# Layer 1's first keys in layer 0's last block, first loads in another order, and layer 1's queries behind feature maps and values

## The chip, the cores and the metric

The kernel runs on one core of one Trainium2 chip. The metric is the device time of one execution in microseconds, the median of several runs. The engines are named as in the profile: PE (TensorE, matmuls), PEld (its weight loads), DVE (VectorE), ACT (ScalarE), POOL (GpSimd) and SP (SyncE, which mostly issues transfers). Each engine works through a list of its own in order; it waits only for semaphores that other engines and transfers raise. Transfers can be issued by SP, by ACT and by POOL, and an issue stands in the list of its engine like any other instruction.

## The reference, cut to what matters

A stack of four layers works on x (8 batches of 256 tokens, width 512), with a context of the same shape. Every layer adds a gated attention over the context and a gated feed-forward part:

```
x = x + tanh(g_xattn[0]) * xattn0(layernorm(x), ctx)      # layer 0
x = x + tanh(g_ffn[0])   * ffn0(layernorm(x))
x = x + tanh(g_xattn[1]) * xattn1(layernorm(x), ctx, ctx) # layer 1
x = x + tanh(g_ffn[1])   * ffn1(layernorm(x))
...                                                       # layers 2 and 3

xattn0: q = w8a8(x, wq);  k = ctx @ wk.T + bk;  v = ctx @ wv.T + bv    # 16 heads of 32
        out = w8a8(softmax(q k / sqrt(32) + mask) v, wo)
        # w8a8 quantises rows of activations and of weights to 8 bits on the fly
ffn0:   8 experts of rank 64; each token uses the one with the largest logit
xattn1: q = x @ Wq.T + bq;  k = ctx @ Wk.T + bk;  v = ctx @ Wv.T + bv  # 16 heads of 32
        q' = relu(q Wqf.T);  k' = relu(k Wkf.T) * mask                 # 64 features a head
        out = (q' (k' v)) / (q' sum(k') + 1e-8)  @ Wo.T + bo           # linear attention
ffn1:   64 experts, 8 for each token, routed; and a shared MLP
```

The keys of layer 1 depend on the context alone and not on x. The change rests on this: they can be computed at any time once the context, Wk and bk are there.

## The kernel before, in words

The 2048 tokens are cut into 4 blocks (NB) of 512, two batches each, and a block into 4 tiles (TB) of 128 tokens. The width of 512 is cut into 4 chunks (KC) of 128. x stays in on-chip memory as 16 tiles (xt). A product of a 128-wide chunk of a 512x512 weight with a block is four matmuls in f32, each in two passes (line 177, helper matmul_k); such a product for all of a block is 16 matmuls, 32 passes. Results land in PSUM, in pools mm (4 buffers), tr (2, for transposes) and ac (2), and are copied out by DVE or ACT.

A scheduler orders the instructions from the order in which the program names them, with their dependencies and the pools' free buffers; so where the code says yield or step(), the author interleaves by hand, and the scheduler moves things from there.

*First loads.* The gates' two small broadcasts and their tanh are the first things on ACT's queue (lines 76 to 79). front() (line 222) then loads wq on SP, wk on ACT, x's first four tiles on SP, the first block's transposed context (load_ctxT, line 85) on ACT, wv and the biases on ACT, wo and the other tiles of x on SP. DVE quantises wq; PE transposes it and, in keys(0) (line 262), multiplies the context with wk; queries(0) (line 281) normalises and quantises x; values(0) follow.

*Layer 0.* Eight batches of attention (attend0, line 429) run one after the other. In each, 16 heads are scored four at a time, exponentiated on ACT, transposed and multiplied with the values. After each head step() (line 409) lets other work into the stream: the projection of the batch before (project), and as many pieces of others(blk) (line 363) as `due` says. others gives the experts of the block before (experts, line 303), and the queries, keys and values of the block behind. The last block has no block behind it, so there is less to interleave, and `due` grows by 0.65 a head there instead of 1.1. After the last head come what is left of the generator, the projection of the last batch, and the experts of the last block, one after the other:

```
            for _ in gen:
                pass
        for _ in proj[0]:
            pass
        for _ in experts(NB - 1, mmtile):
            pass
```

*Layer 1* (middle, line 580, loads its weights at 586 and behind). attend1 (line 657) does for each block: load the context; K, 16 matmuls; the norm of x, its transposes (norm_T), and four adds of the output bias to x on POOL (line 665); Q, 16 matmuls; then for each of the two batches kf, the keys' feature map, 64 small matmuls of 32 rows (line 687), values (8 matmuls for the batch's two tiles), qf, kv, qkv, transposes and the output projection. Here, too, step() gives room to another generator: route1 (line 799), which for every batch finished before normalises x, computes the logits, chooses experts, and writes 16 sets of rows to a table in DRAM with indirect transfers on POOL (line 906).

*Queues.* SP issues weights, contexts, x and masks in order. ACT issues biases, broadcasts and, at the start, wk, the context and wv, between its activations. POOL issues the indirect transfers and computes each norm's power (line 145), the adds of gbo and some more, all in order.

Of the kernel before, what the change touches and what calls it, by code (L numbers as in the profile page):

```python
# [20 lines left out]
P = 128  # L21
# [24 lines left out]
def flamingo_kernel(ctx: ExitStack, tc: tile.TileContext, a):  # L46
# [29 lines left out]
    nc.scalar.dma_start(gate[:, 0:4], a["g_xattn"].partition_broadcast(P))  # L76
    nc.scalar.dma_start(gate[:, 4:8], a["g_ffn"].partition_broadcast(P))
    tg = const.tile([P, 8], F32, tag="tg", name="tg")
    nc.scalar.activation(tg, gate, AF.Tanh)
# [3 lines left out]
    ctxT = {}  # L83

# [137 lines left out]
    def front():  # L222
        isd = 1.0 / float(np.sqrt(HD))
        raw = {"wq0": weight_k("wq0", "wq0")}
        wkT = weight(a["wkT0"], "wk0", eng=nc.scalar).rearrange("p (k o) -> p k o", k=KC)
        for i in range(TB):
            nc.sync.dma_start(xt[i], a["x"][ts(i, P), :])
        load_ctxT(0, "a", nc.scalar)
        wvT = weight(a["wvT0"], "wv0", eng=nc.scalar).rearrange("p (k o) -> p k o", k=KC)
# [3 lines left out]
        gbo = row("bo0", "gbo0")  # L233
        raw["wo0"] = weight_k("wo0", "wo0")
# [68 lines left out]
        def experts(blk, bank):  # L303
            A, Bw = AB
            xns = norm(blk, "f0")
            yield
            xnT = b8.tile([P, KC, BLK], F32, tag="b8", name=f"xnT_f0{blk}")
            for i in range(TB):
                transpose4(xnT[:, :, ts(i, P)], xns[i], f"f0{blk}_{i}")
                if i % 2:  # L310
                    yield
# [51 lines left out]
        def others(blk):  # L363

            if blk + 1 < NB:
                load_ctxT(blk + 1, "a")
            if blk == 0:
                gsw_ps = actile("gsw_ps")
                quantised("wo0", lambda j, s: spread(gsw_ps[:, ts(j, P)], s, f"wo{j}"))
                nc.vector.tensor_scalar(gswo, gsw_ps, tg[:, 0:1], None, ALU.mult)  # L370
                aos.append(wpool.tile([P, 2, 2, C], F32, tag="w", name="aos"))
                yield
                AB.extend([weight_k("A0", "A0"), weight_k("B0", "B0")])

            def tokens():
# [4 lines left out]
                if blk + 1 < NB:  # L380
                    yield from queries(blk + 1, actile)

            def context():
                if blk + 1 < NB:
                    yield from keys(blk + 1, actile)
                    yield from values(blk + 1, actile)

            yield from mix(tokens(), context(), 2)

# [15 lines left out]
        for blk in range(NB):  # L405
# [3 lines left out]
            def step():  # L409
                if proj and next(proj[0], 0) is not None:  # L410
                    proj.pop()
                due[0] += 1.1 if 0 < blk < NB - 1 else 0.65
# [11 lines left out]
        for _ in proj[0]:  # L424
            pass
        for _ in experts(NB - 1, mmtile):
# [153 lines left out]
    def middle():  # L580
        with ExitStack() as st:
# [4 lines left out]
            wk = weight_k("WkT1", "Wk1")  # L586
# [69 lines left out]

            def attend1(blk, step):
                load_ctxT(blk, "b")
                K = b8.tile([P, KC, BLK], F32, tag="b8", name=f"K1_{blk}")
                Q = b8.tile([P, KC, BLK], F32, tag="b8", name=f"Q1_{blk}")  # L660
                for dst, w, bias, src in ((K, wk, bk, ctxT[blk]), (Q, wq, bq, None)):
                    if src is None:
                        _, src = norm_T(blk, "a1")
                        for t in range(blk * TB, blk * TB + TB):
                            nc.gpsimd.tensor_tensor(out=xt[t], in0=xt[t], in1=gbo, op=ALU.add)
                    for j in range(KC):
                        ps = mmtile(f"qk1_{blk}_{j}")
                        matmul_k(ps, [w[:, k, ts(j, P)] for k in range(KC)], [src[:, k, :] for k in range(KC)])
                        nc.scalar.activation(dst[:, j, :], ps, AF.Identity, bias=bias[:, j : j + 1])
                        step()  # L670
                for bb in range(BLK // S):
                    nm = f"{blk}_{bb}"
                    V = la.tile([P, 2, NH, HD + 1], F32, tag="V1", name=f"V1_{nm}")
                    nc.gpsimd.memset(V[:, :, :, HD : HD + 1], 1.0)
                    kf = b8.tile([P, 2, NH * FD], F32, tag="b8", name=f"kf_{nm}")
                    qf = b8.tile([P, NH // 2, S], F32, tag="b8", name=f"qf_{nm}")

                    heads = [slice(HD * r, HD * r + HD) for r in range(4)]
                    ps = [
                        (mm if r < 2 else ac).tile([P, 2, KC, FD], F32, tag="mm" if r < 2 else "ac", name=f"kf_{nm}_{r}")  # L680
                        for r in range(4)
                    ]
                    last = None
                    for lt in range(2):
                        for j in range(KC):
                            for r in range(4):
                                one = nc.tensor.matmul(
                                    ps[r][:, lt, j, :],
                                    K[heads[r], j, ts(bb * 2 + lt, P)],
                                    fm["WkfT1"][heads[r], :],  # L690
                                    start=True,
                                    stop=True,
                                )
                                if last is not None:
                                    behind(one, last, "heads side by side")
                                last = one
                    for r in range(4):
                        for lt in range(2):
                            t = blk * TB + bb * 2 + lt
                            nc.vector.tensor_scalar(  # L700
                                kf[:, lt, :].rearrange("p (j r f) -> p j r f", r=4, f=FD)[:, :, r, :],
# [1083 lines left out]
```

## Time and profile before

| | us |
|---|---|
| median of 3 runs | 2891.76 (2890.22 to 2892.02) |
| the profiled execution | 2896.51 |
| its span, first to last instruction | 2894.5 |
| PE busy in it | 2660.6 |
| DVE busy | 1308.3 |
| POOL busy | 932.3 |
| ACT busy | 698.2 |

The stages in the trace:

| stage | from | to | us |
|---|---|---|---|
| first loads to the first scores | 0 | 51 | 51 |
| layer 0, last block's two batches | 393.9 | 507.7 | 113.8 |
| from the last output transposes to layer 1's first matmul | 507.7 | 563.4 | 55.7 |
| layer 1, block 0 | 563.4 | 650.8 | 87.4 |
| layer 1, block 1 | 650.8 | 760.8 | 110.0 |
| layer 1, block 2 | 760.8 | 877.3 | 116.5 |
| layer 1, block 3 | 877.3 | 995 | about 118 |

The page's lines give for a group of instructions their line in the code, engine, operation, output and inputs, shapes and count. In a timeline the first two numbers are start and length in us, and a bracket names the idle time of that engine just before and what ended it ("issue" if the trace shows nothing that it waited for). In a table of windows each pair is the busy time of an engine and, in brackets, its number of instructions; behind them stand the granted clock of PE (1.00 is full speed), the share of the DMA engines' time and the rate.

### The profile page before, as it was taken

The numbers are of one execution on the slowest core, as the hardware profiler recorded it, in microseconds if no ns is written. First come the engines' busy times: TensorE is split into PE (matmuls) and PEld (weight loads), VectorE is DVE, ScalarE is ACT, GpSimd is POOL, SyncE is SP. The second block draws the span as 40 slices with busy tenths as digits, with TensorE's granted clock in tenths as the row PEclk, the third lists the DMA queues.
The fourth block names the chain that finished last, engine by engine and source line by source line (L and its number), as shares of the span: only waits on it lengthen the run. The fifth ranks groups of instructions, "written<-read, shape, count | busy, mean of one in ns | idle before, by whom it ended". The sixth has DMA issues, their size and how long they took to land. (4 is left out here: it accounts for less than half of the span.)

```text
span 2894.5 us, 29839 instructions
## 1 busy us (share of the span) xinstructions
PE 2660.6 (92%) x10528; PEld 1418.6 (49%) x10543; DVE 1308.3 (45%) x3534; ACT 698.2 (24%) x1565; POOL 932.3 (32%) x840
## 2 busy tenths in 40 slices
PE   7889978898889789999999989999899998799998
PEld 3444544465555435555555434444344434355554
DVE  7666675345545432222222281557666665121111
ACT  2534344011111113333333311122222221111111
POOL 1101020205323335555555410121322233433332
PEclk9999989899899889999999999999999999999999
DMA  5000000210101129999999861112022211488885
GB/s 200 23 4 19 19 34 5 63 37 23 59 23 38 55 67 221 217 218 217 225 214 221 181 226 58 66 62 98 29 88 87 98 15 60 137 274 293 275 272 136
DMA packets 99812, 337.02 MB, mean 116 GB/s; under 512 B 22255, under 2 KB 24687, under 8 KB 91728
## 3 DMA queue, kind: packets, MB, share of 16 engines
q0 software_dynamic: 49344, 160.45, 22.9%
q1 hardware_dynamic: 47440, 169.38, 17.1%
q10 hardware_dynamic: 2880, 5.28, 0.6%
q8 instruction: 85, 1.39, 0.2%
q14 instruction: 63, 0.52, 0.1%
HBM read 284.56 MB, written 69.02 MB: 122 GB/s over the span
## 5 line engine op out<-in xcount | busy, mean ns | idle before, releaser
L177 PE MATMUL gu<-w,eb 128*128 128x352 f32 x1024 | 326.0, 461 | 0.0
L1074 POOL DMA_INDIRECT acc<-eb,who x128 | 204.6, 1598 | 198.2 <-DVE eb L98 166.9
L177 PE MATMUL h2p<-xnT_f,p 128*128 128x512 f32 x512 | 228.0, 601 | 6.0 <-issue 3.9
L177 PEld LDWEIGHTS gu<-w,eb 128*128 128x128 f32 x1024 | 185.6, 191 | 83.2 <-issue 2.3
L177 PE MATMUL o2f<-p,h 128*128 128x512 f32 x512 | 225.6, 595 | 0.7 <-ACT h L1187 0.7
L473 ACT ACTIVATE pr<-pr,n 128x256 f32<-128x256 f32 x256 | 127.9, 501 | 158.1 <-DVE n L468 152.5
L177 PEld LDWEIGHTS h2p<-xnT_f,p 128*128 128x128 f32 x512 | 97.6, 193 | 125.7 <-issue 121.1
L177 PEld LDWEIGHTS o2f<-p,h 128*128 128x128 f32 x512 | 97.0, 191 | 119.2 <-issue 115.0
L1028 POOL DMA_INDIRECT xg<-xnd,who x128 | 134.6, 1051 | 61.1 <-PE ehp L1054 26.8
L906 POOL DMA_INDIRECT table<-pay,rowi x128 | 126.7, 990 | 64.8 <-issue 37.5
L1065 PE MATMUL ed<-w,eb 128*128 128x512 f32 x256 | 120.8, 594 | 0.9 <-DVE eb L1055 0.9
L188 DVE SCALAR_TENSOR_TENSOR x<-o2f,tg,x 128x512 f32<-128x512 f32 x64 | 47.8, 748 | 162.9 <-PE o2f L177 162.9
L98 DVE COPY eb<-ed 128x512 f32<-128x512 f32 x64 | 44.3, 692 | 158.5 <-PE ed L1065 158.5
L161 PEld LDWEIGHTS tr_xg<-ident,xg 128*128 128x128 f32 x656 | 76.4, 142 | 76.2 <-issue 57.0
L1187 ACT ACTIVATE h<-h2p,b 128x512 f32<-128x512 f32 x64 | 43.1, 687 | 290.3 <-PE h2p L177 290.2
L1044 DVE SCALAR_TENSOR_TENSOR eb<-eb,slots,gu 128x176 f32<-128x176 f32 x128 | 50.3, 393 | 139.1 <-ACT eb L1043 77.5
L161 PE MATMUL tr_xg<-ident,xg 128*128 128x128 f32 x656 | 103.4, 281 | 10.3 <-DMA xg<-xnd,who 10.3
L1442 PE MATMUL g_r<-w,xgT 128*128 128x352 f32 x288 | 111.7, 469 | 0.7 <-ACT xgT L100 0.7
L1442 PE MATMUL u_r<-w,xgT 128*128 128x352 f32 x288 | 108.7, 459 | 0.0
L480 PE MATMUL pt<-ident,pr 128*128 128x128 f32 x512 | 88.0, 293 | 19.5 <-ACT pr L473 16.2
L1043 ACT ACTIVATE eb<-gu 128x176 f32<-128x176 f32 x128 | 40.7, 318 | 264.4 <-PE gu L177 264.4
L1465 PE MATMUL d_r<-w,hT_r 128*128 128x512 f32 (+1 forms) x216 | 104.2, 592 | 0.0
(403 smaller groups left out, 4806.2 us busy)
## 6 DMA issues: line engine op xcount, KB each, us to landing
w<-in_w SPq DMA_DIRECT2D x64, 960.0 KB
p<-in_p SPq DMA_DIRECT2D x64, 512.0 KB
xnd<-xn_f SPq DMA_DIRECT2D x32, 256.0 KB
acc<-xnd SPq DMA_DIRECT2D x32, 256.0 KB
more<-acc SPq DMA_DIRECT2D x32, 256.0 KB
wd<-in_wd SPq DMA_DIRECT2D x64, 96.0 KB
x<-in_x SPq DMA_DIRECT2D x16, 256.0 KB
ctxTb<-in_ctxT SPq DMA_DIRECT2D x4, 1024.0 KB
```

Of the source, the lines that this page charges most:

```text
L161: nc.tensor.transpose(ps[:, k, :], src[:, ts(k, P)], ident)
L177: one = nc.tensor.matmul(ps, lhsT[k], rhs[k], start=(k == 0), stop=(k == n - 1))
L188: return nc.vector.scalar_tensor_tensor(xt[i], ps, scale, xt[i], ALU.mult, ALU.add)
L473: nc.scalar.activation(pr[:, nt, :], pr[:, nt, :], AF.Exp, bias=n16[:, nt, h : h + 1], scale=-1.0, accum_out=s16[:, nt, h : h + 1],)
L480: nc.tensor.transpose(pt_ps[:, lt, nt, :], pr[:, nt, ts(lt, P)], ident)
L906: one = nc.gpsimd.indirect_dma_start(out=table[:, :], out_offset=bass.IndirectOffsetOnAxis(ap=row_i[:, i, j : j + 1], axis=0), in_=pay[:, ...
L1028: nc.gpsimd.indirect_dma_start(out=xg, out_offset=None, in_=xnd[:, :], in_offset=bass.IndirectOffsetOnAxis(ap=who[:, c : c + 1], axis=0), ...
L1044: nc.vector.scalar_tensor_tensor(self.h, self.h, slots[:, c, 1:2], gu[:, I1 : 2 * I1], ALU.mult, ALU.mult)
L1065: one = nc.tensor.matmul(ps[n], t.hT[rows, k, :], wd[k][rows], start=(k == 0), stop=(k == 1))
L1074: nc.gpsimd.indirect_dma_start(out=acc[n][:, :], out_offset=bass.IndirectOffsetOnAxis(ap=who[:, t.c : t.c + 1], axis=0), in_=t.x, in_offse ...
L1442: nc.tensor.matmul(ps[:, 0:I3], xTt[:, k, :], wgu[k][:, g, :], start=(k == 0), stop=(k == KC - 1))
L1465: one = nc.tensor.matmul(ps, hT[:cn, n, :], wd[n][:cn], start=(n == 0), stop=(n == 2))
```

## The change

1. First loads: the gates' transfers and tanh become a function, called behind the loads of the biases. The context of block 0 moves from ACT's queue to the head of SP's, ahead of wq; wv follows wk at once on ACT.
2. In layer 0's last block, others() loads layer 1's Wk, a copy of its bk and the contexts of blocks 0 and 1. Between the heads run layer 1's keys of block 0 and a quarter of those of block 1, and the first two pieces of the last block's experts, whose norm is now done in two halves; `due` grows by 0.9 a head in that block. The rest of block 1's keys stands between the pieces of the last projection and behind it, and then come the experts.
3. Layer 1's attend1 takes the keys of blocks 0 and 1 from there. In every block the order becomes: keys (blocks 2 and 3 only), norm, feature map and values of the first batch (context1, which holds V, kf's 64 small matmuls and the values as attend1 had them), transposes, POOL's adds, Q, and then the rest.

The arithmetic stays the same. What is new is one small transfer (the copy of bk) and one more power on POOL (the norm in halves).

```diff
     gate = const.tile([P, 8], F32, tag="gate", name="gate")
-    nc.scalar.dma_start(gate[:, 0:4], a["g_xattn"].partition_broadcast(P))
-    nc.scalar.dma_start(gate[:, 4:8], a["g_ffn"].partition_broadcast(P))
     tg = const.tile([P, 8], F32, tag="tg", name="tg")
-    nc.scalar.activation(tg, gate, AF.Tanh)
+    def gates():
+        nc.scalar.dma_start(gate[:, 0:4], a["g_xattn"].partition_broadcast(P))
+        nc.scalar.dma_start(gate[:, 4:8], a["g_ffn"].partition_broadcast(P))
+        nc.scalar.activation(tg, gate, AF.Tanh)
...
     def front():
+        wkT = weight(a["wkT0"], "wk0", eng=nc.scalar).rearrange("p (k o) -> p k o", k=KC)
+        load_ctxT(0, "a")
         raw = {"wq0": weight_k("wq0", "wq0")}
-        wkT = weight(a["wkT0"], "wk0", eng=nc.scalar).rearrange("p (k o) -> p k o", k=KC)
+        wvT = weight(a["wvT0"], "wv0", eng=nc.scalar).rearrange("p (k o) -> p k o", k=KC)
         for i in range(TB):
             nc.sync.dma_start(xt[i], a["x"][ts(i, P), :])
-        load_ctxT(0, "a", nc.scalar)
-        wvT = weight(a["wvT0"], "wv0", eng=nc.scalar).rearrange("p (k o) -> p k o", k=KC)
...
         gbo = row("bo0", "gbo0")
+        gates()
...
-        def experts(blk, bank):
+        def experts(blk, bank, halves=1):
             A, Bw = AB
-            xns = norm(blk, "f0")
-            yield
             xnT = b8.tile([P, KC, BLK], F32, tag="b8", name=f"xnT_f0{blk}")
-            for i in range(TB):
-                transpose4(xnT[:, :, ts(i, P)], xns[i], f"f0{blk}_{i}")
-                if i % 2:
-                    yield
+            n = TB // halves
+            for half in range(halves):
+                xns = norm_of(range(blk * TB + half * n, blk * TB + half * n + n), f"f0{blk}_{half}_")
+                yield
+                for i in range(n):
+                    transpose4(xnT[:, :, ts(half * n + i, P)], xns[i], f"f0{blk}_{half * n + i}")
+                    if i % 2:
+                        yield
...
             if blk + 1 < NB:
                 load_ctxT(blk + 1, "a")
+            else:
+                first1["wk"] = weight_k("WkT1", "Wk1")
+                first1["bk"] = columns("bk1", KC, "bk1a")
+                for b in range(2):
+                    load_ctxT(b, "b")
...
                 if blk + 1 < NB:
                     yield from queries(blk + 1, actile)
+                else:
+                    for _ in range(2):
+                        yield next(last_experts)

             def context():
                 if blk + 1 < NB:
                     yield from keys(blk + 1, actile)
                     yield from values(blk + 1, actile)
+                else:
+                    yield from keys1(0, actile)
+                    yield next(last_keys)
...
+        def keys1(b, bank):
+            K1 = first1["K", b] = b8.tile([P, KC, BLK], F32, tag="b8", name=f"K1_{b}")
+            for j in range(KC):
+                ps = bank(f"k1ps{b}_{j}")
+                matmul_k(
+                    ps, [first1["wk"][:, k, ts(j, P)] for k in range(KC)], [ctxT[b][:, k, :] for k in range(KC)]
+                )
+                nc.scalar.activation(K1[:, j, :], ps, AF.Identity, bias=first1["bk"][:, j : j + 1])
+                yield
+        last_experts = experts(NB - 1, mmtile, 2)
+        last_keys = keys1(1, mmtile)
...
-                due[0] += 1.1 if 0 < blk < NB - 1 else 0.65
+                due[0] += (0.65, *(NB - 2) * (1.1,), 0.9)[blk]
...
-        for _ in proj[0]:
+        for n, _ in enumerate(proj[0]):
+            if n == 1:
+                next(last_keys)
+        next(last_experts)
+        for _ in last_keys:
             pass
-        for _ in experts(NB - 1, mmtile):
+        for _ in last_experts:
             pass
...
+            def context1(blk, bb, K, step):
...
+                return kf, V
             def attend1(blk, step):
-                load_ctxT(blk, "b")
-                K = b8.tile([P, KC, BLK], F32, tag="b8", name=f"K1_{blk}")
+                if ("K", blk) in first1:
+                    K = first1["K", blk]
+                else:
+                    load_ctxT(blk, "b")
+                    K = b8.tile([P, KC, BLK], F32, tag="b8", name=f"K1_{blk}")
+                    for j in range(KC):
+                        ps = mmtile(f"k1_{blk}_{j}")
+                        matmul_k(ps, [wk[:, k, ts(j, P)] for k in range(KC)], [ctxT[blk][:, k, :] for k in range(KC)])
+                        nc.scalar.activation(K[:, j, :], ps, AF.Identity, bias=bk[:, j : j + 1])
+                        step()
+                xns = norm(blk, "a1")
+                first = context1(blk, 0, K, step)
+                xnT = b8.tile([P, KC, BLK], F32, tag="b8", name=f"xnT_a1{blk}")
+                for i in range(TB):
+                    transpose4(xnT[:, :, ts(i, P)], xns[i], f"a1{blk}_{i}")
+                for t in range(blk * TB, blk * TB + TB):
+                    nc.gpsimd.tensor_tensor(out=xt[t], in0=xt[t], in1=gbo, op=ALU.add)
                 Q = b8.tile([P, KC, BLK], F32, tag="b8", name=f"Q1_{blk}")
-                for dst, w, bias, src in ((K, wk, bk, ctxT[blk]), (Q, wq, bq, None)):
-                    if src is None:
-                        _, src = norm_T(blk, "a1")
-                        for t in range(blk * TB, blk * TB + TB):
-                            nc.gpsimd.tensor_tensor(out=xt[t], in0=xt[t], in1=gbo, op=ALU.add)
-                    for j in range(KC):
-                        ps = mmtile(f"qk1_{blk}_{j}")
-                        matmul_k(ps, [w[:, k, ts(j, P)] for k in range(KC)], [src[:, k, :] for k in range(KC)])
-                        nc.scalar.activation(dst[:, j, :], ps, AF.Identity, bias=bias[:, j : j + 1])
-                        step()
+                for j in range(KC):
+                    ps = mmtile(f"q1_{blk}_{j}")
+                    matmul_k(ps, [wq[:, k, ts(j, P)] for k in range(KC)], [xnT[:, k, :] for k in range(KC)])
+                    nc.scalar.activation(Q[:, j, :], ps, AF.Identity, bias=bq[:, j : j + 1])
+                    step()
                 for bb in range(BLK // S):
                     nm = f"{blk}_{bb}"
+                    kf, V = context1(blk, bb, K, step) if bb else first
```

## The prediction

> **What bounds the kernel now.** I read first the busy shares, then the windows by stage, the timeline of TensorE (PE) where a window showed idle time or a low clock, and last the waits of one block.
>
> The busy shares:
>
> ```profile
> PE 2660.6 (92%) x10528; PEld 1418.6 (49%) x10543; DVE 1308.3 (45%) x3534; ACT 698.2 (24%) x1565; POOL 932.3 (32%) x840
> ```
>
> PE is the bound. The change adds no matmul and removes none, so it can only move work into stretches where PE idles or runs at half clock, or out of them. Those stretches are what counts. The windows by stage (length, then busy time and instructions of PE, its weight loads, DVE, ACT, POOL; then granted clock, DMA share, GB/s):
>
> ```profile
> 394.00:451.00 57.00, 42.43 (x287) 25.62 (x293) 34.45 (x120) 23.05 (x76) 10.53 (x8) 0.85 0.02 6
> 451.00:508.00 57.00, 49.62 (x302) 26.20 (x295) 31.98 (x109) 25.21 (x81) 5.49 (x8) 0.94 0.00 1
> 508.00:520.00 12.00, 4.38 (x17) 1.81 (x16) 6.35 (x16) 0.59 (x1) 4.41 (x4) 0.59 0.51 166
> 520.00:530.00 10.00, 6.42 (x36) 5.61 (x36) 4.25 (x9) 1.17 (x2) 1.62 (x2) 0.64 0.05 18
> 530.00:540.00 10.00, 10.00 (x29) 5.75 (x28) 3.36 (x13) 0.23 (x1) 0.00 (x0) 0.66 0.00 0
> 651.00:761.00 110.00, 96.12 (x533) 58.47 (x532) 60.72 (x254) 13.81 (x24) 39.77 (x41) 0.92 0.12 39
> 761.00:877.00 116.00, 98.00 (x532) 60.29 (x531) 57.50 (x251) 13.81 (x24) 39.53 (x41) 0.88 0.09 28
> ```
>
> See: layer 0's batches 6 and 7 (394-508) have nothing left to fill with and PE is idle for 57 - 42.4 + 57 - 49.6 = 22 us; the tail behind them (508-540) is idle for 11.2 us at a clock near 0.6; layer 1's blocks idle for 14 to 18 us each.
>
> **The change part by part.** The profiled execution took 2896.51 us (span 2894.5, 2.0 around it), 4.75 us over the median of the runs, 2891.76; differences in us worked out in it are carried to the median as they are. A measurement of this kernel can tell about 0.2%, 5.8 us, from no change.
>
> *1. First loads (0-51 us).* The timeline of ACT and its queue, and of PE, from which lines are left out:
>
> ```profile
> 8.31 1.28 ACT L79 ACT_TABLE_LOAD   x1 [8.31 <-DMA gate<-in_g_ffn]
> 8.37 0.34 ACTq L87 DMA_DIRECT2D ctxTa<-in_ctxT  x1
> ```
>
> ```profile
> 16.05 2.08 PE L177 MATMUL k0ps<-ctxTa,wk 128*128 128x512 f32 x2 [3.51 <-DMA ctxTa<-in_ctxT]
> ...
> 20.58 12.99 PE L177 MATMUL k0ps<-ctxTa,wk 128*128 128x512 f32 x28
> ...
> 36.31 1.03 PE L177 MATMUL q0ps<-qxT,qT 128*128 128x512 bf16 x3
> ```
>
> ACT stands at its tanh until the gates land, and the context load is queued behind it: issued at 8.37, landed at 16.0. After, SP issues it first. It and wk, 2 MB at the rate seen (49, 209 and 234 GB/s in the first three 2 us, then about 340), land near 8.4, so the keys can start 8 us earlier. But q0ps at 36.31 waits for something else: DVE's chain from wq (landed 7.35) through quantising it, x's norm (xn ready 24.2) and quantising x. wq comes behind them: 3 MB are in near 10.9. The gates are issued behind gbo; I put them at 21 (20 to 22). Three queues feel it. ACT, in order: the copy of the second transposed quarter of wq stands behind the tanh, and only two PSUM buffers hold such transposes, so PE's fourth set waits; the keys end near 28.5 instead of 33.4. DVE: gbo's scaling by tanh (0.48 us, at 29.19 before) now stands ahead of x's norm in the built program, so xn goes from 24.2 to about 25.9 and q0ps from 36.3 to about 36.9. SP: x0 to x3 pass behind ctxT, 1 MB, about 3 us later, which is inside that 25.9. Then PE has almost only transposes from 28.5 to 36.9; if it drops to half clock there, the query matmuls (36.3 to 39.8) take up to 3.4 more. I take +2; bounds -2 (DVE's chain not late, keys gone from in front of the transposes) and +6.
>
> The Trainium skill, "TensorE: Matmul & The Clock Gate", Part 1 ("Why this matters for your kernels" sums it up), says that an idle gap of about 3 us puts PE back to half clock, and Part 4 that transposes don't count as busy. It speaks against this part. The row 508-520, idle or on transposes at 0.59, agrees with it; by the rule the head would be 0.6 + 3.4 = +4.0 instead of +2.
>
> *2. Keys of layer 1's blocks 0 and 1 in layer 0.* They are 2 x 13.90 us of PE in layer 1 (the row of 760.79 below is another such block). In the order of the built program 25 of the 32 matmuls (0.86 us each, two passes) stand before batch 7's last output transposes, 7 behind them.
>
> Batches 6-7, 113.8 us from 393.9 to 507.7: PE busy 92.0. Clocks 0.85 and 0.94 mean about 24 us at half clock, which at 80% busy wastes 9.6, so the work is 82.4 at full clock. Added: 25 x 0.86 = 21.5 and 1.1 of transposes for the first half of the experts' norm. That is 105. The two full blocks before (132-394) are busy for 237.7 of 262 us at 0.97 and 0.93: about 230 of full-clock work, 88%. At 88%, 105 takes 119.3: +5. Bounds: 95% gives 110.5, -3; 86% gives +8; if the heads' chain through ACT and DVE holds and nothing hides, +22. I take +5, as the full blocks are the nearest rows. The loads of Wk, bk (a second copy) and two contexts, 3 MB, move here on SP and ACT; the DMA share is 0.02, and they need buffers that are free by about 370, so they cost nothing; if a context came late, PE would wait up to the 8 us that 1 MB took at the start.
>
> The tail, 507.71-563.40 (55.7 us). PE's timeline:
>
> ```profile
> 511.49 1.03 PE L212 MATMUL trq_o<-identb,q_o 128*128 128x128 bf16 x8 [3.34 <-DVE q_o L206]
> 513.02 3.19 PE L177 MATMUL wo<-qT,qoT 128*128 128x512 bf16 x7 [0.49 <-DVE qoT L98]
> 523.58 3.84 PE L161 MATMUL tr_f<-ident,xn_f 128*128 128x128 f32 x16 [7.37 <-DVE xn_f L149]
> ```
>
> A chain: quantise, transpose, project, add on POOL, norm, transpose, then experts. The order after puts 7 keys matmuls (6.0) into these waits and, since half of the norm's tiles are ready, half the logits and three of the first expert matmuls. The list at full clock: output transposes 0.4, keys 6.0, quantised transposes 0.8, projection 1.7, logits 3.7, first expert matmuls 13.8, f transposes 1.1, h transposes 2.0, second ones 13.9 = 43.4. With 2.6 of idle left: 46, so -9.7. Bounds -12 (no idle) and -5 (half the idle stays). One more rstd on POOL (0.73) is in that. Where POOL is still adding, the second half's norm is late by as much.
>
> Layer 1 loses the two blocks: -27.8, certain unless something else becomes late there.
>
> *3. Queries behind feature maps and values.* PE's timeline of block 2, and PE's waits in block 1:
>
> ```profile
> 760.79 13.90 PE L177 MATMUL qk<-ctxTb,Wk 128*128 128x512 f32 x32
> 774.52 1.04 PE L161 MATMUL tr_f<-ident,xn_f 128*128 128x128 f32 x8
> 779.04 1.30 PE L161 MATMUL tr_a<-ident,xn_a 128*128 128x128 f32 x8 [3.49 <-DVE xnT_f L98]
> ...
> 789.62 15.92 PE L177 MATMUL qk<-xnT_a,Wq 128*128 128x512 f32 x32 [4.38 <-issue]
> ```
>
> ```profile
> PE kf L687 <- issue: 8.1, 8, 1.9
> ```
>
> Every block has two bursts of 16 table writes on POOL, 22 and 20 us long (656.3-678.3 and 705.7-725.8 in block 1). From about 11.5 us into a burst until 2 us after it, PE, DVE and ACT start small instructions only every 0.7 us or so, while large matmuls are not slowed. (a) In the first bursts tr_f to Q takes 10.4, 15.1 and 11.5 us for 5.0 of work (664.5, 774.5, 891.0). (b) In the second ones the 64 small matmuls of kf take 13.5 us or more instead of 2.0, and half clock behind costs values 2.75 more: about 14.2 a stall.
>
> After, block 1 has no keys; its norm and POOL's four adds of gbo (1.26 each) stand ahead of the table writes, so the second half of the burst lies on Q's large matmuls: gain 5 (0 to 7). Blocks 2 and 3 keep keys first; then kf, values, logits fill the wait ahead of tr_a: worth up to 10.6 each if kf (2 us from about 775.6) ends before the stall (about 778); if it is caught, it loses 4.7 each instead. It is close, so I weigh both by one half: (-10.6 + 4.7) / 2 = -3 each, -6 for both. The second bursts start about 8 us later against the work, on kf of the second batch again: I leave them at 0, +-4 a block, and take off 3 of the gain for block 0 and for the shift of the adds (DVE waited 5.76 and 3.03 us for POOL at 677.6 and 790). -5 - 6 + 3 = -8, bounds -28 (both waits filled, second bursts eased too) and +18 (kf caught everywhere).
>
> Layers 2 and 3 aren't touched and move along.
>
> **Sum**: +2 + 5 - 9.7 - 27.8 - 8 = -38.5: 2891.8 - 38.5 = 2853 (2858 in a profiled execution).
>
> **The rivals.**
> *The bursts are dodged.* For it: block 0, which has no burst, runs at clock 1.00 with 86.0 of 88 us busy. Against: tables are still written, 96 of them in these blocks. Layer 1 then gives -28 instead of -8: 2833.
> *The heads don't hide the keys.* For it: PE's longest wait in 394-508 is for ACT's probabilities, and ACT gets six more keys to copy out there. Against: blocks 1-2 hide as much and more. +22 in place of +5, and kf caught in blocks 2 and 3 (+9.4 in place of -6): -38.5 + 17 = -21 with the first alone, -6 with both: 2871 to 2886, about 2877.
> *Slower: a stall in new places.* One mechanism: kf, feature maps and small transposes of the new order fall into both bursts of blocks 1 to 3. Price 14.2 us each. The parts outside layer 1's blocks sum to -30.5, so it decides from 30.5 us of added stall: two more (28.4) leave it about equal, three give -30.5 + 42.6 = +12, 2904. For it: three first bursts that now hold kf. Against: in blocks 2 and 3 keys still cover the first 14 us.
> *The first loads don't do what they say, or do.* If the earlier context did bring the queries forward by the 4.9 us that the keys end earlier, the head gives -5: 2846. It lies inside the forecast's own range.
>
> **How the numbers follow.** Forecast 0.52 (own range 2840 to 2866: the bounds of the four terms drawn together), dodged 0.15, not hidden 0.18, slower 0.11, and 0.04 for the gain and the stalls cancelling. 2824 leaves about 0.04 below; 2884 leaves the slower case and most of the even one above. Faster by over 0.2% 0.85, within 0.04, slower 0.11.
>
> **What would show it.** Part 1: first k0ps near 8 to 9 us, q0ps at 36 to 38, gates near 21. Part 2: last o near 513 instead of 507.7; first layer 1 matmul about 46 us behind it; no 13.90 us of keys in blocks 0 and 1. Part 3: in blocks 2 and 3 whether kf's 64 matmuls stay together, and Q's start less than 15 us behind tr_f. The prediction is wrong if batches 6-7 lengthen by over 10 us or if kf shows waits by issue in more than three places.

## The result and the profile after

The change makes no difference that can be measured: 2893.83 us median against 2892.97 for the kernel before, a ratio of 1.0003 with a 95% interval from 0.9992 to 1.0013. 2853 had been predicted. On a second chip the ratio was 1.0014 [1.0004, 1.0023], 3.2 us slower.

The two profiled executions differ by 7.6 us (span 2894.5 and 2886.9), more than the medians do; single executions of either kernel lie up to 11 us apart. So a stage is read from several traces here. The stages, from the end of the last matmul y of layer 0 and of the output projections wo of layer 1:

| us | first scores | layer 1 starts | block 0 | block 1 | block 2 | block 3 |
|---|---|---|---|---|---|---|
| before | 51.0 | 563.6 | 87.4 | 110.0 | 116.5 | 112.9 |
| after | 52.9 | 562.7 | 84.9 | 97.6 | 119.3 | 117.4 |
| before, second chip | 50.3 | 562.8 | 87.4 | 110.2 | 109.6 | 109.6 |
| after, second chip | 53.8 | 563.5 | 84.7 | 97.4 | 120.2 | 119.9 |

What follows layer 1's attention takes 1903 to 1905 us of the span in all of them. Layer 0 takes on 27.5 us of keys and ends within 1 us of when it did. Layer 1 loses those 27.5 us of work, but its four blocks are only 7.6 us shorter on the first chip, and 5.4 us longer on the second.

The shares of the changed kernel's page, and its windows at the end of layer 0 and by layer 1's blocks (length; busy time and instructions of PE, its loads, DVE, ACT, POOL; clock, DMA share, GB/s):

```profile
PE 2665.4 (92%) x10528; PEld 1417.6 (49%) x10543; DVE 1295.2 (45%) x3535; ACT 697.1 (24%) x1565; POOL 932.9 (32%) x841
```

```profile
394.00:451.00 57.00, 46.71 (x276) 27.02 (x271) 32.12 (x114) 23.77 (x76) 9.31 (x8) 0.88 0.02 5
451.00:508.00 57.00, 51.73 (x282) 26.47 (x285) 32.52 (x113) 25.50 (x82) 5.75 (x5) 1.00 0.00 1
508.00:520.00 12.00, 12.00 (x75) 6.40 (x76) 5.21 (x10) 2.82 (x5) 0.46 (x4) 1.00 0.02 4
520.00:530.00 10.00, 9.95 (x46) 5.53 (x46) 4.84 (x14) 1.96 (x3) 4.65 (x4) 1.00 0.66 213
530.00:540.00 10.00, 8.17 (x37) 4.60 (x35) 6.00 (x19) 0.82 (x2) 1.08 (x2) 1.00 0.00 0
```

```profile
562.70:647.60 84.90, 78.62 (x479) 48.73 (x478) 46.40 (x157) 11.45 (x19) 13.83 (x13) 0.92 0.11 38
647.60:745.20 97.60, 82.04 (x501) 52.24 (x502) 50.26 (x241) 10.73 (x20) 33.41 (x36) 0.91 0.14 44
745.20:864.50 119.30, 102.11 (x534) 61.73 (x533) 54.74 (x254) 13.81 (x24) 39.46 (x41) 0.89 0.09 27
```

The holes in layer 0's tail are closed: from 508 to 540 PE is busy for 30.1 of 32 us, at full clock. The windows 394 to 508 are idle for 15.6 us instead of 22. Block 0 of layer 1, which ran at full clock with 86 of 88 us busy, is now idle for 6.3 us and at 0.92; blocks 1 and 2 are idle for 15.6 and 17.2 us.

PE's timeline shows where. (tr_a and tr_f are transposes of the normalised x, for the queries q and for route1; k and v are keys and values, kf is the keys' feature map, lgp_f are route1's logits.) In block 0:

```profile
564.58 7.13 PE L180 MATMUL v<-Wv,ctxTb 128*128 128x512 f32 x16
571.55 1.04 PE L164 MATMUL tr_a<-ident,xn_a 128*128 128x128 f32 x8
576.18 1.97 PE L164 MATMUL tr_a<-ident,xn_a 128*128 128x128 f32 x8 [3.60 <-DVE xnT_a L101]
578.83 16.02 PE L180 MATMUL q<-xnT_a,Wq 128*128 128x512 f32 x32 [0.68 <-ACT xnT_a L103]
```

The queries still wait for the norm, now behind 9 us of kf and values instead of 13.9 us of keys. The second half of the transposes waits 3.6 us for a copy on DVE, which has kf's eight copies and the values' ahead of it; then the queries run partly at half clock (16.02 for 14.0). In block 2:

```profile
745.05 13.90 PE L180 MATMUL k<-ctxTb,Wk 128*128 128x512 f32 x32
758.79 1.04 PE L164 MATMUL tr_f<-ident,xn_f 128*128 128x128 f32 x8
759.75 1.10 PE L710 MATMUL kf<-WkfT,K 32*128 32x64 f32 x26
761.63 0.42 PE L710 MATMUL kf<-WkfT,K 32*128 32x64 f32 x2 [0.78 <-issue]
...
772.54 5.21 PE L180 MATMUL v<-Wv,ctxTb 128*128 128x512 f32 x6 [0.44 <-issue]
```

The first batch's kf starts 9.2 us into the burst of table writes, is caught 10.4 us into it, and takes 12.4 us instead of 2.0, and values run at half clock behind it.

### The profile page after: what moved, and what is told of

Read it like the earlier page. It is cut to its first block, busy times and chain, and to the rows that moved or that the text cites. A ratio compares the mean times of both kernels' runs of the same rounds, so it can differ in the third digit from the quotient of the medians.

```text
span 2886.9 us, 29835 instructions
## 1 busy us (share of the span) xinstructions
PE 2665.4 (92%) x10528; PEld 1417.6 (49%) x10543; DVE 1295.2 (45%) x3535; ACT 697.1 (24%) x1565; POOL 932.9 (32%) x841
## 5 line engine op out<-in xcount | busy, mean ns | idle before, releaser
L1097 DVE SCALAR_TENSOR_TENSOR eb<-eb,slots,gu 128x176 f32<-128x176 f32 x128 | 50.3, 393 | 138.7 <-ACT eb L1096 87.7
L504 DVE CUSTOM_DVE_ANT_0 pr<-s,mask 128x256 f32<-128x256 f32 x256 | 96.8, 417 | 11.1 <-PE s L484 7.7
```

The source lines that it names most:

```text
L504: one = nc.vector.tensor_tensor_reduce(pr[:, nt, :], ps[r][:, nt, :], mask[:, nt, :], -1.0, -LOW, ALU.add, ALU.min, n16[:, nt, h : h + 1],)
L1097: nc.vector.scalar_tensor_tensor(self.h, self.h, slots[:, c, 1:2], gu[:, I1 : 2 * I1], ALU.mult, ALU.mult)
```

## Experiments

Two theories stood against each other. Theory 1: the keys taken out of layer 1 had covered the norm's chain there, so their time was not on the path. Theory 2: the new order puts small matmuls under the table writes, and that takes the gain. Each part was run alone first. The diffs show only the lines that decide.

**The first loads alone** (the gates' loads and front()'s order as in the change, nothing else).

```diff
+        wkT = weight(a["wkT0"], "wk0", eng=nc.scalar).rearrange("p (k o) -> p k o", k=KC)
+        load_ctxT(0, "a")
         raw = {"wq0": weight_k("wq0", "wq0")}
```

> Only the first loads in the changed order, on the kernel before. The theory (the queries wait for the chain from wq over x's norm, which the earlier context does not touch): first scores 1 to 3 us later than 51.0, the whole +2 us (0 to +4). The rival (the earlier context brings the first block forward): first scores near 46, the whole -5 us.

2890.84 against 2887.26: 1.0011 [1.0002, 1.0020], +3.6 us; first scores at 54.1 and layer 1's start at 566.1 in the profile. On the second chip the kernel before has its first scores at 50.3 and the changed one at 53.8, the same step. The rival falls; the theory's size holds, at the upper end of its 0 to +4.

**The keys alone** (part 2, layer 1's order as before).

```diff
+                K = first1.get(("K", blk))
+                products = []
+                if K is None:
+                    load_ctxT(blk, "b")
+                    K = b8.tile([P, KC, BLK], F32, tag="b8", name=f"K1_{blk}")
+                    products.append((K, wk, bk, ctxT[blk]))
```

> Layer 1's keys of blocks 0 and 1 in layer 0's last block, the first loads and layer 1's order as before: in those blocks the norm now stands in front of the queries with no keys beside it. Theory 1 (in layer 1 the keys had covered the norm's chain from the last addition to x, so that taking them out uncovers it): layer 0 with its tail about 0, block 0 shorter by 3 to 5 us only instead of 13.9, block 1 by 5 to 10, blocks 2 and 3 as before; the whole -8 to -15 us. Theory 2 (the changed order in layer 1 is what gives the gain back, by small matmuls under the table writes): block 0 and 1 shorter by 12 to 14 each, the whole near -28.

2887.72 against 2887.26, 1.0002 [0.9993, 1.0011]: nothing. Layer 1 starts at 562.9; block 0 takes 87.7 (87.4 before), block 1 110.7; with the keys in place, in the run of the first loads on the same chip, they take 87.4 and 110.1. Both theories expected some gain. Split by batches, block 0's first shortens from 57.6 to 51.3 and its second grows from 29.8 to 36.4; block 1's change from 66.9 and 43.3 to 59.5 and 51.2. What a first batch gains, the second gives back. In block 1 a new stall has a part in it: the first batch's kf takes 12.5 us there instead of 2.0. PE's timeline of block 0's first batch:

```profile
568.53 1.94 PE L162 MATMUL tr_a<-ident,xn_a 128*128 128x128 f32 x8 [5.62 <-DVE xn_a L150]
570.80 1.88 PE L162 MATMUL tr_a<-ident,xn_a 128*128 128x128 f32 x8 [0.34 <-DVE xnT_a L99]
573.36 14.00 PE L178 MATMUL qk<-xnT_a,Wq 128*128 128x512 f32 x32 [0.68 <-ACT xnT_a L101]
```

**The order alone** (part 3, all keys in layer 1).

```diff
+                xns = norm(blk, "a1")
+                first = context1(blk, 0, K, step)
```

> Only layer 1's queries behind feature maps and values; all four blocks compute their keys in layer 1. Theory 1 (cover of the norm gone): block 0 still has its keys, so it keeps its 87 us; blocks 1 to 3 each +3 to +5 us as in blocks 2 and 3 of the changed kernel, because the first batch's feature map now stands under the table writes; the whole +9 to +15. Theory 2 (the order alone gives back everything): +25 or more.

2918.32, 1.0108 [1.0093, 1.0124]: +31 us. Block 0 87.7 as expected, blocks 1 to 3 120.4, 119.6 and 118.2, 9 to 10 each above the 109.5 to 110.1 of the run of the first loads on the same chip. Theory 1's size was too small by more than half; the order alone costs what theory 2 said. But the parts don't add up: alone they cost 3.6, 0.5 and 31 us, together 1 to 3. Most of the difference is block 1, which takes 97.4 to 97.6 us with its keys moved and the new order, and 110.7 and 120.4 with only one of the two. PE's waits in blocks 1 and 2 with the order alone:

```profile
PE kf L674 <- issue: 18.0, 24, 1.8
PE lgp_f L177 <- DVE kf L687: 7.4, 2, 4.6
```

**The table writes held back**, on both kernels, until the last batch's norm. They then stand ahead of the experts, so only the stages are compared.

```diff
-                    for j in range(K1):
-                        one = nc.gpsimd.indirect_dma_start(
+                    if q < 2 * NB - 1:
+                        later.append((row_i, pay, i))
+                    else:
+                        table_rows(row_i, pay, i)
...
+                for rows in later:
+                    table_rows(*rows, last_rstd[0])
```

> The kernel before, with the table writes of batches 0 to 6 held back until attention of layer 1 has ended (they then stand in front of the routed experts, so the whole time grows by up to 140 us; what counts is the time from the first to the last matmul of layer 1's attention, 427 us before). If the table writes are what slows the small instructions of blocks 1 to 3: the 64 small matmuls of kf take 2.0 us everywhere and the blocks shorten from 110, 116.5 and 113 to 88 to 92 each, 427 to about 360. If they are not (a limit of the matmuls or of the waits between the engines): within 15 us of 427.

> The changed kernel with the same writes held back. If the table writes are the cause: kf takes 2.0 us everywhere, block 0 as in the changed kernel (85, since it has no table writes), block 1 about 75 to 78, blocks 2 and 3 88 to 90 each, the attention of layer 1 419 to about 335; the changed kernel then keeps some 22 to 27 us of gain in layer 1 that it loses under the writes. If not: within 15 us of 419, and no more gain than the 7.7 us that the changed kernel shows there.

Whole times 2929.43 and 2913.60. Blocks of the kernel before: 87.4, 90.7, 90.7, 90.8, 359.6 in sum; of the changed one: 84.9, 77.1, 91.6, 91.8, 345.4. The 64 matmuls of kf take 2.01 everywhere, as here in block 2 of the changed kernel:

```profile
738.37 1.04 PE L166 MATMUL tr_f<-ident,xn_f 128*128 128x128 f32 x8
739.34 2.01 PE L712 MATMUL kf<-WkfT,K 32*128 32x64 f32 x64
741.28 2.84 PE L182 MATMUL v<-Wv,ctxTb 128*128 128x512 f32 x6
```

Against the first profiled pair (426.8 and 419.2) that is 67 and 74 us less, but on another chip, where a single execution of the kernel before, with its bursts, took 2850.77 us; it has no profile here, so how large the stalls are on that chip is not known, and this pair alone doesn't show that the writes make them. The pacing below does, on one chip. Without the bursts the change gains 14.2 us in layer 1, not the 22 to 27 expected: block 1 is shorter by all of its keys (13.6), block 0 by 2.5, and the new order costs 1 in each of blocks 2 and 3.

**The writes paced**: about 1.3 at each step, each waiting for the latest large matmul, with both kernels unchanged beside them.

```diff
             def step():
                 next(gen, None)
+                pace[0] = min(pace[0] + 1.3, 2.0)
+                while later and pace[0] >= 1.0:
+                    pace[0] -= 1.0
+                    table_row(*later.pop(0), latest[0])
```

> The kernel before, unchanged, for its profile on the same chip as the next three. If the stalls under the table writes belong to the kernel and not to one chip, the 64 matmuls of kf take 13 to 14 us in the second batch of blocks 1 to 3 again and the whole stays within 0.2% of the other runs of the kernel before on this chip.

> The changed kernel, unchanged, on the same chip. If stalls as large as before: equal to the kernel before within 0.2%. If the stalls are smaller on this chip than where it was profiled first, the changed kernel is faster by up to the 14 us by which the runs with the writes held back differed in layer 1.

> The changed kernel with the table writes of batches 0 to 6 not in bursts of 16 but about 1.3 at a step, each waiting for the latest large matmul. If what throttles the small instructions is the density of the writes (a reserve of about 100 instructions, refilled between the writes): kf near 2 to 4 us everywhere, layer 1's attention 419 to 350 to 375, the whole -40 to -65 us. If every write slows them, however spread: the same sum of stall in other places, the whole within 10 us of the changed kernel.

> The same pacing on the kernel before. If the density counts: layer 1's attention 427 to 365 to 385, the whole -40 to -60 us; the paced changed kernel would then be faster than this by 14 us or more, the gain that the changed kernel lost under the bursts. If not: within 10 us of the kernel before.

Against the 2888.60 of the kernel before on this chip: before 2887.29, after 2891.75 (1.0014), paced before 2844.10 (0.9854 [0.9837, 0.9870]), paced after 2828.91 (0.9798 [0.9781, 0.9814]). So bursts of writes are the cause of most of the stall: layer 1's attention takes 375.6 instead of 416.8 us in the kernel before and 360.3 instead of 422.2 in the changed one. Each write by itself is not. Pacing changes the density of the writes and also moves them beside large matmuls; the runs do not separate the two. Under pacing the changed kernel is 15.2 us faster than the other: the gain that the bursts had taken. In the changed kernel's block 2, PE and POOL while kf runs, in 3.1 us instead of 12.4 or 10.2, with a write starting inside it:

```profile
744.22 2.08 PE L710 MATMUL kf<-WkfT,K 32*128 32x64 f32 x51
746.62 0.69 PE L710 MATMUL kf<-WkfT,K 32*128 32x64 f32 x13 [0.31 <-issue]
```

```profile
745.20 1.23 POOL L855 DMA_INDIRECT table<-pay,rowi  x1 [0.30 <-issue]
746.44 2.50 POOL L762 TENSOR_TENSOR x<-x,gbo 128x512 f32<-128x512 f32 x2
752.09 0.99 POOL L855 DMA_INDIRECT table<-pay,rowi  x1 [3.14 <-PE lgp_f L180]
```

**Which block's keys are worth moving**, paced and with the old first loads: both, only block 1's, only block 0's.

```diff
-                for b in range(2):
-                    load_ctxT(b, "b")
+                load_ctxT(1, "b")
...
-                    yield from keys1(0, actile)
                     yield next(last_keys)
```

(and with 0 for 1, keys1(0, mmtile) as last_keys, for the third)

> The paced changed kernel with the first loads as in the kernel before. From the first loads alone (+3 us): 2 to 4 us less than the paced changed kernel, first scores at 50 to 51 again; near 2826, against the kernel before -60 to -65. If the first loads mattered only beside the rest: no difference from the paced changed kernel's -59.7.

> As paced_no_loads, with only block 1's keys computed in layer 0; block 0's stay in layer 1 and cover the norm there. Theory 1 (block 0's keys were cover, and taking them out gains 2.5 us there, whatever it costs in layer 0): block 0 87 again instead of 84.6, block 1 84 as in paced_no_loads, and layer 0 has 13.9 us less to hide, so layer 1 starts up to 6 us earlier; the whole 0 to -4 against paced_no_loads. Rival (layer 0 hides both for nothing, and block 0's keys cost their 13.9 in layer 1): layer 1 starts at the same time, the whole +3 to +14.

> The mirror: only block 0's keys in layer 0, block 1's in layer 1. Theory 1: block 0 85, block 1 96 to 97 instead of 84, layer 0 as in paced_one_block; the whole 10 to 12 us longer than paced_one_block. Rival (a block's keys are worth the same wherever they stand): within 3 us of paced_one_block.

| paced | whole | layer 1 starts | block 0 | block 1 | blocks 2, 3 |
|---|---|---|---|---|---|
| both | 2829.32, 0.9762 [0.9745, 0.9780] | 561.5 | 84.7 | 83.9 | 96.2, 96.2 |
| block 1's | 2834.89, 0.9782 [0.9763, 0.9801] | 554.5 | 94.5 | 82.9 | 97.9, 96.3 |
| block 0's | 2826.72, 0.9755 [0.9738, 0.9773] | 549.8 | 79.9 | 96.4 | 96.2, 96.3 |

Theory 1 fails in this: block 1's keys alone are the worst choice, not the best. Block 0's second batch takes 34.9 to 36.6 wherever block 1's keys are gone, and 29.8 wherever they are not; so moving block 1's keys costs 5 to 7 us one block earlier. And layer 0 takes one block of keys and still ends 9 to 13 us earlier than before (549.8 and 554.5 against 563.2, paced), but the second block pushes its end back by 7 to 12. That these two differ by 4.7 with the same number of keys says little: with the same layer 0 as in the third row, later runs start layer 1 at 553.4 and 554.7. With the old first loads the paced kernel is no faster than with the new ones (2829.32, 2828.91), but on another chip, so their 3.6 us stay unconfirmed here.

**What makes that second batch long, and whether only the stages that gain add up.** First block 0's keys and the new order in block 0 only, under the bursts and paced; then both blocks' keys with POOL's adds behind the queries.

```diff
-                first = context1(blk, 0, K, step)
+                first = context1(blk, 0, K, step) if ("K", blk) in first1 else None
```

> Bursts as in the kernel before, first loads as before; only block 0's keys in layer 0, and only block 0 in the new order; blocks 1 to 3 as in the kernel before. If the stage lengths seen so far add up: layer 1 starts 13 us earlier (about 550), block 0 takes 80 instead of 87.4, its second batch 29.8, blocks 1 to 3 their 110 each: the whole -18 to -22 us. Rival (the bursts take whatever is gained ahead of them): within 6 us of the kernel before.

> The same with the table writes paced. Blocks 1 to 3 in the old order were 95.4 to 97.2 paced, in the new one 96.2 to 96.4: no difference from paced_block0 above 2 us, so 2825 to 2828.

> paced_no_loads with POOL's four adds of the output bias behind the queries instead of ahead of them. If the adds of block 1, moved forward into block 0's second batch, hold DVE and through it PE there: that batch 30 to 31 us instead of 36.4, the whole -5 us. If it is the norm alone (DVE's own instructions): 34 to 36 again and the whole within 2 us of paced_no_loads.

Block 0 alone: 2868.51 against 2887.19, 0.9937 [0.9921, 0.9954], -18.7 us with the bursts as they are; layer 1 starts at 553.4, the blocks take 79.5, 110.0, 109.5 and 109.5. The stages add up, but for layer 1's start (550 was expected; the 549.8 that this rested on was one execution). Half of the gain lies in layer 0, which ends 9.4 us earlier although it takes on keys; no run has the rest of part 2 (the norm in halves, the experts' first pieces, `due`) without any keys, so what the keys have to do with that half is open. Paced: 2826.87 (0.9791 [0.9775, 0.9807]), as expected. The late adds told nothing: 2826.68, but the scheduler left the adds where they were, at 622.37. So they were made to wait:

```diff
+                    tc.add_manual_dep(
+                        one.ins, latest[0].ins.name,
+                        mybir.DependencyInfo(mybir.DependencyClass.Sync, mybir.DependencyReason.DATA),
+                        reason="behind the queries")
```

> paced_late_adds with each add waiting for the last matmul of its block's queries, so that block 1's adds can't run in block 0's second batch. If the adds hold DVE and through it PE there: that batch 30 to 32 us instead of 34.9, the whole 3 to 5 us less than paced_late_adds. If it is the norm of block 1 on DVE: 34 to 35 again, the whole within 2 us.

> paced_no_loads with only block 1's adds behind its queries. By the stage lengths of paced_adds_wait and paced_no_loads: block 0 80 instead of 84.7, blocks 2 and 3 96 each, the whole 3 to 5 us less than the 2827 to 2829 of the paced kernels with both blocks' keys moved, so 2822 to 2826. If the gain is lost later: 2827 to 2830.

Waiting in all blocks: block 0's second batch 31.0 instead of 34.9, but blocks 2 and 3 102.6 and 102.5 instead of 96, the whole 2834.95 (0.9813 [0.9795, 0.9831]). Waiting in block 1 only: that batch 31.0 again, block 0 80.7, the whole 2827.44 (0.9764 [0.9745, 0.9783]), its single times from 2822.3 to 2832.4, too far apart to tell the last 4 us. The mechanism is shown by POOL's line, DVE's and PE's in the changed kernel, and by DVE's and PE's with the adds waiting:

```profile
624.39 5.60 POOL L762 TENSOR_TENSOR x<-x,gbo 128x512 f32<-128x512 f32 x4 [0.66 <-DVE xn_a L152]
623.76 2.41 DVE L152 TENSOR_SCALAR xn_a<-x,mv_a,rstd_a 128x512 f32<-128x512 f32 x3 [1.12 <-POOL rstd_a L148]
627.50 1.35 DVE L877 TENSOR_TENSOR sc<-sco,eb 128x128 f32<-128x128 f32 x1
```

```profile
632.29 5.60 PE L819 MATMUL qkv<-kv,qf 128*128 128x66 f32 x32 [0.67 <-DVE best_f L589]
637.68 2.15 PE L164 MATMUL tr_ao<-ident,ao 128*128 128x128 f32 x8
```

```profile
620.49 1.46 DVE L150 TENSOR_SCALAR xn_a<-x,mv_a,rstd_a 128x512 f32<-128x512 f32 x3 [1.12 <-POOL rstd_a L146]
622.92 0.29 DVE L902 TENSOR_TENSOR sc<-sco,eb 128x128 f32<-128x128 f32 x1
```

```profile
627.61 3.74 PE L822 MATMUL qkv<-kv,qf 128*128 128x66 f32 x32
631.18 0.60 PE L162 MATMUL tr_ao<-ident,ao 128*128 128x128 f32 x4
```

With no keys in block 1, its norm and POOL's adds run in the batch before, where route1's small DVE steps are. Beside the adds the same DVE instructions take 2.41 instead of 1.46 us and 1.35 instead of 0.29; so qkv, the product of queries and the keys' and values' state, comes late and then runs at half clock (5.60 instead of 3.74). The adds account for 3.9 us of the batch; the last 1.1 us over 29.9 may be the norm's, which no run shows alone.

The best versions beat the kernel before by 2.0 to 2.5%, of which pacing alone gives 1.5%. They lie within 3 us of each other: block 0's keys alone, paced (2826.7 to 2826.9), has the least in it.

## Why the prediction was wrong

- **First loads, +2: right in mechanism and within its bounds, small in size.** First scores 1.9 us later in the profiled pair, 3.5 in the second chip's, +3.6 us for the whole alone; that is nearer the +4.0 that the prediction named beside it. The working held: keys at 8.67 (near 8.4 worked out), q0ps at 36.20 (36.9). The changed kernel's first matmuls, and ACT's tanh:

```profile
8.67 6.65 PE L180 MATMUL k0ps<-ctxTa,wk 128*128 128x512 f32 x10 [8.67 <-DMA wk<-in_wkT]
...
36.20 0.59 PE L180 MATMUL q0ps<-qxT,qT 128*128 128x512 bf16 x1
37.00 1.49 PE L180 MATMUL q0ps<-qxT,qT 128*128 128x512 bf16 x3 [0.22 <-issue]
```

```profile
18.56 0.21 ACT L81 ACTIVATE tg<-gate 128x8 f32<-128x8 f32 x1 [0.73 <-DMA gate<-in_g_ffn]
```

  The gates landed 2.5 us sooner than the 21 taken. The q0ps matmuls take about 0.5 us each instead of 0.34, so the half clock named there as a risk came. The Trainium skill, "TensorE: Matmul & The Clock Gate", Part 4, says that a transpose doesn't count as PE-busy the same way; the trace agrees, for from 25.9 to 36.2 PE had only transposes and small products, and the clock granted from 30 to 40 us was 0.50. But PE was also idle for about half of that stretch, so the run doesn't tell which of the two did it.
- **Batches 6-7 +5, tail -9.7: the first term was mis-sized.** From batch 6's first scores to the last output transposes it took 125.4 us instead of 113.8, +11.6 (+11.4 on the second chip): over the 10 that the prediction had named as a sign of being wrong. It took its 88% from the full blocks, "about 230" of 262; counted as it counted batches 6 and 7, they hold 226, 86%, which is its own +8, and the 105 us of work ran at 84%. The tail takes 44.6 instead of 55.7, -11.1 (-13.4 on the second chip), a little better than forecast. The sum is +0.5 and -2.0 where -4.7 was forecast. Layer 1's start moved by -0.9 and +0.7 where -2.7 was forecast; on the first chip that is luck in part, for the batches before were 3.2 us faster, which nothing had forecast.
- **"Layer 1 loses the two blocks: -27.8, certain unless something else becomes late there": this step failed.** Something did: the sentence priced the removed work and not what it covered. Even with the writes held back the two blocks give 2.5 + 13.6 = 16.1 (paced, on one chip, 2.7 + 13.6), and in the old order under the bursts nothing at all. Block 0's first batch gives 7.6, for its norm chain is bare; its second batch takes 5.1 back, for block 1's norm and adds move into it. Nearly all that is missing of the 27.8 is missing in block 0.
- **The new order, -8: this step failed, in sign.** The stall was read as a time, 11.5 us after a burst begins, so blocks 2 and 3 were a coin toss and block 1 a gain. It set in 10.4 and 10.6 us after the burst's begin in blocks 2 and 3, so kf was caught in both, and 3.1 us after it in block 1. kf showed waits by issue in five places, over the three that the prediction had named. In the profiled pair the order cost 1.2 in block 1 (against the 13.6 that its keys are worth), 2.8 and 4.5 in blocks 2 and 3; on the second chip 0.8, 10.6 and 10.3.
- **The slower rival** named the mechanism and the price: it decided from 30.5 us of added stall and put two more stalls at "about equal". With two new stalls (kf in blocks 2 and 3) the result was equal. But its fixed part, -30.5, held the same 27.8, so that its even case came out is in part luck. The chance of 0.04 on no change was far too low: the terms of both signs shared one cause and were not summed as a case.

Of the 38.5 us forecast, in the first profiled pair 11.7 went with the lost cover, 16.5 with the order and its stalls (-8 forecast, 1.2 + 2.8 + 4.5 measured) and 1.8 in layer 0; 0.9 came behind layer 1, and 7.6 were there. That the medians show none of these 7.6 lies in the spread between executions.

## What to carry to other kernels

Before work is counted as gained where it is taken out, find what runs beside it: the same queue of matmuls that looks like pure cost may be the cover of a norm's chain, and what stands behind it on other engines moves forward into someone else's time. If a stall is tied to another engine's burst, look at where it sets in at more than two places before naming what it counts, and test it by spreading the burst; here that was worth 44.5 us on the kernel before and 62.8 on the changed one, the change itself nothing under the bursts and 15.2 us under pacing. And run the parts alone and in pairs: of three, two cost and one gave nothing, they did not add up, and a subset of them gave 18.7 us.

## What the runs showed of the hardware that was not expected

The stall under POOL's bursts of indirect writes does not begin at a fixed time: it came 3 to 12 us after a burst's first write, and soonest where the instructions came densest. In the changed kernel's block 1 the burst begins at 693.2, and the windows behind it are:

```profile
693.20:694.50 1.30, 1.30 (x4) 0.35 (x2) 1.17 (x9) 0.00 (x0) 0.97 (x1) 1.00 0.00 0
694.50:696.50 2.00, 1.81 (x46) 1.73 (x46) 1.99 (x9) 0.00 (x0) 1.69 (x2) 1.00 0.03 1
696.50:700.00 3.50, 1.61 (x11) 1.59 (x11) 0.30 (x3) 0.00 (x0) 2.58 (x4) 0.86 0.03 3
700.00:704.00 4.00, 1.96 (x9) 1.79 (x9) 0.00 (x0) 0.00 (x0) 3.08 (x4) 0.50 0.02 1
```

and in the kernel before, where the burst begins at 705.7:

```profile
705.70:709.00 3.30, 2.80 (x24) 2.36 (x23) 2.57 (x17) 0.00 (x0) 2.67 (x3) 1.00 0.02 1
709.00:716.50 7.50, 7.13 (x17) 2.96 (x16) 3.64 (x15) 0.59 (x1) 5.67 (x7) 1.00 0.04 4
716.50:717.70 1.20, 1.14 (x31) 0.98 (x30) 0.00 (x0) 0.00 (x0) 0.89 (x2) 1.00 0.02 1
717.70:721.00 3.30, 0.85 (x5) 0.66 (x5) 1.86 (x4) 0.00 (x0) 2.43 (x3) 1.00 0.02 1
```

All engines together start 50 a microsecond for two microseconds, and are held to 8 and then 5 to 6 from 3.3 us after the burst's first write; in the kernel before, with 7 to 20 a microsecond until kf starts, the same comes after 12 us. A reserve that is refilled at a rate would do this: 119 instructions (16 + 103) in 3.3 us and 186 (67 + 56 + 63) in 12.0 give 67 in 8.7 us, an estimate of 8 a microsecond and a reserve of some 90. Two places always give two such numbers, and a third does not bear them out: in the changed kernel's blocks 2 and 3 kf is first caught after 140 instructions in 10.4 and 10.6 us, where these numbers would allow over 170, and behind that 10 to 13 a microsecond still start. So neither time nor the count of all instructions alone is shown to set it off. What in the chip holds them is open; whether the recording of the instructions has a part in it was not tried.

The chips differ. The kernel before took 2887 to 2897 us at the median wherever it ran several times, and on one more chip, in the single execution beside the held-back writes, 2850.77. The paced forms of the changed kernel stayed within 2827 to 2835 on four chips.
